# Layer 0 of a four-layer convolution stack: affine in the first pass, v multiplied with pixels on partitions, 32x32 turns, eight-tile output product

## The chip, the core and the metric

The kernel runs on one core of a Trainium2 chip. A core has five engines that run side by side, each with its own in-order queue: TensorE (PE; it loads weights and streams a moving operand past them, and writes to PSUM), VectorE (DVE), ScalarE (ACT), GpSimd (POOL) and SyncE (SP, here only a queue that starts DMAs). They meet only at semaphores. PSUM is the memory that TensorE writes to; SBUF is the working memory, with 128 partitions; HBM holds tensors between passes. The metric is the time of one execution on the device in microseconds (us), lower is better.

## What is computed

The input is a batch of 4 images with 48 channels and 256 x 256 pixels, in float32. Each of four layers adds a block to its input, `x = x + block(groupnorm(x))`. The change is in layer 0:

```python
hidden = _conv2d(x, w_hidden, b_hidden)                       # 48 -> 288 channels, 1x1
qkv = _conv2d(hidden, w_dw, b_dw, groups=C6, padding='SAME')  # 3x3, each channel alone
q, k, v = jnp.split(qkv, 3, axis=1)                           # 96 channels each
q_fft, k_fft = rfft2(q_patch), rfft2(k_patch)                 # 8x8 patches
out = irfft2(q_fft * k_fft)
mu  = jnp.mean(out, axis=1, keepdims=True)                    # over the 96 channels
var = jnp.var(out, axis=1, keepdims=True)
normed = (out - mu) / jnp.sqrt(var + EPS) * gamma + beta
return _conv2d(v * normed, w_out, b_out)                      # 96 -> 48 channels
```

Layers 1 and 2 are a gated convolution with a mask on the spectrum of 8x8 patches, layer 3 is a pooled gate. They are the same in both kernels.

## The kernel before

Layer 0 (the function `layer0`) works on strips of 16 image rows: 4 images x 16 strips are 64 steps. It goes over all strips twice.

**First pass (q and k).** A step n does, in the order of the source: `mixed(n)` (L377 on), the hidden product, 16 groups of eight matmuls, each group copied from PSUM into the tile `z` by ScalarE and VectorE in turn (L396); `arrange(n+1)` and `load(n+2)` on GpSimd, which bring the next strips; `attend(n-2)`; and `convolve(n)`, the 3x3 taps as matmuls (L408) whose results ScalarE copies (L463) and SP sends out to be rearranged into patches. `attend` handles the strip of two steps before, in two halves r = 0 and 1: spectra of q (`queries`, L512) and of k, multiplied on VectorE (`keys`, L517), the inverse transform (`inverse`, L527), copied into the tile `o` (L531). Then the normalization over channels: `centre(r)` sums on VectorE (L542), scales the sum (L543) and subtracts the mean on GpSimd (L544); `scale(r)` squares on ScalarE (L549), sums on VectorE (L551, L552), takes the power -1/2 on GpSimd (L553), multiplies on GpSimd (L554) and stores the strip to HBM as `kept` (L555). `centre(0)` stands between two units of `attend`; the rest is put between the groups of `convolve`: the dictionary that `attend` returns names, by pair (m, q), what follows the copy of group q of part m. Two things decide the order on an engine's queue: normally a planner orders the instructions before the run by readiness and source order, and `keep_in_program_order` (called `here` or `pin`) ties an instruction behind the one in front of it on its engine.

**Second pass (v).** A step n does `mixed(n)` for the 96 channels of v (8 groups), `arrange(n+1)`, then for strip n-1: `normalized` turns the kept strip with TensorE so that channels lie on partitions (L652), and ScalarE applies gamma and beta while copying (L657); `times_v` turns v in the same way (L669) and multiplies on VectorE (L675); `project` is the product with `w_out` (L685), added to the input strip `xt` with the bias on VectorE (L690), followed by the statistics for the next layer's norm (L694) and the store (L699). `convolve_v(n)` (L408, copy L639) stands between them. `load_kept` (L632, on SP) fetches the kept strip, two buffers; `load` (L335, on GpSimd) fetches an input strip, three buffers. A PSUM tile of two banks is used throughout, with four of them in rotation.

Of the kernel before, what the change touches and what calls it, by code (L numbers as in the profile page):

```python
# [17 lines left out]
C = 48  # L18
# [155 lines left out]
def conv_stack_kernel(ctx: ExitStack, tc: tile.TileContext, t: dict):  # L174
# [71 lines left out]
    def layer0():  # L246
# [8 lines left out]
        kept = [dram.tile([2, 128, C2, 16], F32, tag=f"n_{n}", name=f"n_{n}") for n in range(N)]  # L255
# [15 lines left out]
        class Strips:  # L271
# [104 lines left out]
            def mixed(self, n):  # L376
# [5 lines left out]
                to = self.z[0:PX].rearrange("p c (h u j) -> p h c u j", h=2, u=2)  # L382
                for u in range(2):
                    for j0 in range(0, NJ, per):
# [10 lines left out]
                        copy = nc.scalar.copy if (j0 // per) % 2 == 0 else nc.vector.tensor_copy  # L395
# [19 lines left out]
        with ExitStack() as st:  # L415
# [32 lines left out]
            qk = Strips("qk", 0, 2, 1, wp, sb, psum, ("f", 2), 1)  # L448
            patches = {}
# [38 lines left out]
            def attend(n):  # L488
# [30 lines left out]
                def inverse(i):  # L519
                    r, ch = units[i]  # L520
                    f = fs.pop(i)
                    if ch == 0:
                        os_[r] = sb.tile([128, C2, 16], F32, tag="o", name=f"o_{n}_{r}", bufs=2)
                    ps = qk.ps2(f"o_ps_{n}_{i}")
                    for e in range(2):
# [6 lines left out]
                        os_[r].rearrange("p (e c) q -> p e (c q)", e=2)[:, :, 384 * ch : 384 * ch + 384],  # L532
                        ps[:, :, 0:384],
                    )

                over = lambda v: v.rearrange("p (c q) -> p c q", c=1).to_broadcast([128, C2, 16])
                by_q = lambda v: v.rearrange("p c q -> p q c")
                small_ = lambda k, r: sb.tile([128, 16], F32, tag=k, name=f"{k}_{n}_{r}", bufs=2)

                def centre(r):  # L540
                    mu = small_("mu", r)
                    here(nc.vector.tensor_reduce(mu, by_q(os_[r]), AX.X, ALU.add))  # L542
                    nc.vector.tensor_scalar(mu, mu, 1.0 / C2, None, ALU.mult)  # L543
                    here(nc.gpsimd.tensor_tensor(os_[r], os_[r], over(mu), ALU.subtract))  # L544

                def scale(r):
                    o = os_[r]
                    sq = sb.tile([128, C2, 16], F32, tag="f", name=f"sq_{n}_{r}", bufs=2)
                    here(nc.scalar.activation(sq, o, AF.Square))  # L549
                    var = small_("var", r)  # L550
                    here(nc.vector.tensor_reduce(var, by_q(sq), AX.X, ALU.add))  # L551
                    nc.vector.tensor_scalar(var, var, 1.0 / C2, LN_EPS, ALU.mult, ALU.add)  # L552
                    here(nc.gpsimd.tensor_tensor(var, var, neg_half, ALU.pow))  # L553
                    nc.gpsimd.tensor_tensor(o, o, over(var), ALU.mult)  # L554
                    nc.gpsimd.dma_start(kept[n][r], o)  # L555
# [3 lines left out]
                for i in range(4):  # L559
# [9 lines left out]
                    (1, 0): lambda: scale(1),  # L569
# [31 lines left out]
        with ExitStack() as st:  # L601
# [3 lines left out]
            w_out = wp.tile([HC, 64], F32, tag="l0_w_out", name="l0_w_out")  # L605
            nc.gpsimd.memset(w_out, 0.0)

            affine = wp.tile([HC, 3], F32, tag="l0_affine", name="l0_affine")
            nc.gpsimd.memset(affine, 0.0)
            for h in range(2):  # L610
                at, ch = slice(64 * h, 64 * h + C), slice(C * h, C * h + C)
                nc.scalar.dma_start(w_out[at, :C], t["l0_w_out"][ch])
                for k, name in enumerate(("l0_gamma", "l0_beta")):
                    nc.scalar.dma_start(affine[at, k : k + 1], t[name][0:1, ch].rearrange("o c -> c o"))
                nc.scalar.dma_start(affine[at, 2:3], t["l0_b_out"])
            v = Strips("v", 2 * C2, 1, 0, wp, sb, psum, ("nt", 4), 3)

            ss = [wp.tile([128, 64, 64], F32, tag=f"s{i}", name=f"s_v_{i}") for i in range(2)]
            for s in ss:
                nc.gpsimd.memset(s[:, :, 48:64], 0.0)  # L620
# [5 lines left out]
            for w in ws:  # L626
                nc.gpsimd.memset(w[:, :, C:64, :], 0.0)
# [788 lines left out]
```

## Time and profile before

| | us |
|---|---|
| time, median of 3 runs (12357.9 to 12379.25) | 12371.74 |
| the profiled execution | 12404.2 |
| its span | 12402.4 |
| TensorE matmul busy | 11483.6 (93%) |
| VectorE busy | 8003.2 (65%) |
| ScalarE busy | 5857.8 (47%) |
| GpSimd busy | 3566.2 (29%) |
| first pass of layer 0, first hidden product to last | 129.8 to 2949.9 |
| second pass of layer 0, the same | 3099.6 to 4942.8 |

The profile records one execution. A row of a group names the line of the kernel, the engine, the operation and the tiles, and gives its busy time and the mean duration of one instruction; "PEld" is TensorE's weight load, which overlaps the matmuls. Each matmul of the source appears as two instructions. The timeline lists instructions in order of start, neighbours of one kind merged ("x2"), with the idle time in front of them and what ended it. The clock is that which the chip granted TensorE, as a share of full speed.

### The profile page before, as it was taken

Reading aid. Unit: us, or ns where it says so; the run is one execution under the profiler, and the core shown is the slowest. Engines: PE = TensorE matmul, PEld = TensorE weight load, DVE = VectorE, ACT = ScalarE, POOL = GpSimd, SP = SyncE. Lnnn points to the kernel's source line nnn. Section 1 sums busy time; section 2 is a strip of 40 time slices with the busy share of each in tenths; the row PEclk is TensorE's granted clock in tenths of the full one; section 3 lists DMA queues with packets and bytes.
Section 4 is the critical chain, followed back from the end, with each engine's and each line's share of the span. In section 5 each row is a group of like instructions: output and inputs, shape, how many; then the busy total and the mean of one; then the engine's idle time right before and its main releaser. Section 6 shows DMA issues by size and latency. Waiting matters only on the chain. (4 is left out here: it accounts for less than half of the span.)

```text
span 12402.4 us, 457165 instructions
## 1 busy us (share of the span) xinstructions
PE 11483.6 (93%) x209364; PEld 9013.2 (73%) x209364; DVE 8003.2 (65%) x8422; ACT 5857.8 (47%) x7294; POOL 3566.2 (29%) x4300
## 2 busy tenths in 40 slices
PE   5789999997999999999999999999999999999975
PEld 3567777775888888677777777777777777777764
DVE  4667666665444444576666666666766666766778
ACT  2355555554434334444444444444444444444456
POOL 3456666665222222212112112111111121121111
PEclk9899999998999999999999999998999999999987
DMA  6666666665444444455554555554555545555556
GB/s 165 196 206 215 211 216 213 211 217 173 114 118 115 115 112 113 92 118 113 118 118 100 116 116 114 114 116 88 117 109 115 117 100 112 117 115 112 117 142 198
DMA packets 379730, 1707.67 MB, mean 138 GB/s; under 512 B 100193, under 2 KB 102098, under 8 KB 281810
## 3 DMA queue, kind: packets, MB, share of 16 engines
q1 hardware_dynamic: 203016, 907.70, 27.6%
q0 software_dynamic: 130176, 630.91, 21.5%
q10 hardware_dynamic: 44618, 139.81, 4.8%
q8 instruction: 1651, 27.05, 0.9%
q14 instruction: 269, 2.20, 0.1%
HBM read 832.52 MB, written 584.91 MB: 114 GB/s over the span
## 5 line engine op out<-in xcount | busy, mean ns | idle before, releaser
L996 PEld LDWEIGHTS c_ps<-z,d 100*64 100x64 f32 x76032 | 2354.6, 140 | 501.5 <-issue 183.1
L996 PE MATMUL c_ps<-z,d 100*64 100x64 f32 x76032 | 2461.2, 224 | 139.8 <-DVE res L1041 58.9
L1002 ACT ACTIVATE g<-c_ps 128x512 f32<-128x512 f32 x1188 | 686.8, 596 | 3114.8 <-PE c_ps L996 3064.9
L927 DVE TENSOR_TENSOR yf<-y_ps,mask 128x768 f32<-128x768 f32 x1536 | 1375.7, 952 | 688.7 <-PE y_ps L923 688.6
L923 PE MATMUL y_ps<-w_in,f 49*128 49x96 f32 x24576 | 1487.9, 277 | 17.3 <-issue 11.5
L923 PEld LDWEIGHTS y_ps<-w_in,f 49*128 49x128 f32 x24576 | 1422.3, 190 | 56.7 <-issue 15.0
L1003 DVE TENSOR_TENSOR g<-g,c_ps 128x512 f32<-128x512 f32 x1188 | 793.1, 684 | 975.4 <-ACT g L1002 974.7
L974 POOL DMA_DIRECT2D z<-z x384 | 197.6, 515 | 3839.7 <-ACT z L967 3739.2
L949 PE MATMUL z_ps<-yf,dft 64*64 64x512 f32 x9216 | 1099.1, 604 | 7.2 <-DVE yf L927 5.6
L967 ACT COPY z<-z_ps 64x1024 f32<-64x1024 f32 x1024 | 1074.8, 1075 | 34.1 <-DVE z L967 10.1
L959 ACT COPY z<-z_ps 64x512 f32<-64x512 f32 x1536 | 857.9, 611 | 230.5 <-PE z_ps L949 209.7
L1007 DVE STREAM_TRANSPOSE g<-g 128x2048 f32<-128x2048 f32 x396 | 911.2, 2301 | 4.9
L1033 PE MATMUL xo_ps<-g,w_out 24*64 24x512 f32 x12288 | 846.4, 599 | 28.7 <-ACT z L967 28.1
L408 PEld LDWEIGHTS c_ps_qk<-z_qk,d_qk 109*64 109x64 f32 x24576 | 785.1, 139 | 50.5 <-issue 38.2
L389 PE MATMUL h_ps_qk<-w_qk,xn_qk 49*108 49x192 f32 x8192 | 739.6, 336 | 77.0 <-DVE z_qk L396 68.7
L967 DVE COPY z<-z_ps 64x1024 f32<-64x1024 f32 x512 | 619.3, 1210 | 296.6 <-PE z_ps L949 274.4
L408 PE MATMUL c_ps_qk<-z_qk,d_qk 109*64 109x64 f32 x24576 | 795.9, 224 | 11.9 <-issue 7.9
L500 PE MATMUL f_ps<-t,l_fft 64*94 64x384 f32 x4096 | 753.2, 504 | 27.3 <-ACT f L512 21.1
L389 PEld LDWEIGHTS h_ps_qk<-w_qk,xn_qk 49*108 49x108 f32 x8192 | 685.9, 176 | 116.7 <-DVE z_qk L396 92.2
L544 POOL TENSOR_TENSOR o<-o,mu 128x1536 f32<-128x1536 f32 x128 | 443.4, 3464 | 1079.5 <-DVE mu L543 812.5
L1041 DVE TENSOR_TENSOR res<-xo_ps,res 112x1024 f32<-112x1024 f32 x512 | 615.2, 1222 | 186.8 <-PE xo_ps L1033 159.2
L1033 PEld LDWEIGHTS xo_ps<-g,w_out 24*64 24x64 f32 x12288 | 301.0, 131 | 562.3 <-issue 220.3
(205 smaller groups left out, 17192.2 us busy)
## 6 DMA issues: line engine op xcount, KB each, us to landing
z<-z SPq DMA_DIRECT2D x1152, 203.9 KB
t<-s SPq DMA_DIRECT2D x512, 384.0 KB
t<-t SPq DMA_DIRECT2D x256, 768.0 KB
n<-o POOLq DMA_DIRECT2D x128, 768.0 KB, 5.0
kept<-n SPq DMA_DIRECT2D x128, 768.0 KB
xf<-x ACTq DMA_DIRECT2D x256, 384.0 KB
res<-x POOLq DMA_DIRECT2D x248, 384.0 KB, 6.2
x<-res POOLq DMA_DIRECT2D x248, 384.0 KB, 4.3
```

Of the source, the lines that this page charges most:

```text
L389: nc.tensor.matmul(ps[0:PX, h, nch * j : nch * j + nch], self.xn[at, u, j0 + j].rearrange("p r c -> p (r c)"), self.w1[at, self.c_first : ...
L408: nc.tensor.matmul(ps[64 * e : 64 * e + 64, k // 8, 64 * (k % 8) : 64 * (k % 8) + 64], self.d[:, 96 * m + c, :], self.z[:, 96 * m + c, :], ...
L500: nc.tensor.matmul(ps[0:94, e, 0:384], fft[at, 0:94], patches[n, m, r][at, rp, 24 * ch : 24 * ch + 24, :].rearrange("p c u -> p (c u)"), s ...
L923: first(i + j == 0, nc.tensor.matmul(ps[:, i, 96 * j : 96 * j + 96], f[at, 4 * h + j, :], w_in[at, m, :], start=True, stop=True,))
L927: pin(nc.vector.tensor_tensor(y[:, :, :, 4 * h : 4 * h + 4], ps[:, :, 0:384].rearrange("p i (j c) -> p c i j", j=4), mask[:, m].rearrange( ...
L949: first(q == 2 and p + v == 0, nc.tensor.matmul(to[64 * v : 64 * v + 64], dft[at, 1, at], y[at, c0 : c0 + 16].rearrange("p c i j -> p (c i ...
L959: pin(nc.scalar.copy(columns(p, 48 * v + 32, 48 * v + 48), last[64 * v : 64 * v + 64, p].rearrange("p (c i j) -> p c i j", i=2, j=16),))
L967: pin(copy(columns(p, 48 * v, 48 * v + 32), ps[64 * v : 64 * v + 64].rearrange("p q (c i j) -> p (q c) i j", i=2, j=16),))
L996: first(v + k == 0, nc.tensor.matmul(ps[p0 : p0 + 64, v, f0 : f0 + nj], d[rows, HID * v + 48 * m + c, :], z[rows, us, 48 * v + c, 1 : NP + ...
L1003: pin(nc.vector.tensor_tensor(to, to, of[:, 1], ALU.mult))
L1007: pin(nc.vector.transpose(flat, flat))
L1033: first(i + k == 0, nc.tensor.matmul(ps[h][k // 2][64 * i : 64 * i + 64, k % 2, :], w_out[at, m, :], gs[m][at, j0 : j0 + 16].rearrange("p ...
```

## The change

In the first pass the tile `o` is laid out as [half of the channels, pixel group, channel] instead of [channel, pixel group], so that the sums run over neighbouring elements; each sum is made in two halves and added. `scale` no longer multiplies. A new function `affine` does what was left and what the second pass did with gamma: 16 instructions of VectorE per half multiply `o` by the power and by gamma, GpSimd adds beta, and then the strip is stored. The dictionary has four entries instead of two.

In the second pass v is multiplied as it leaves PSUM, with pixels on partitions, by the kept strip (now fetched in that layout, by eight DMAs instead of two, three buffers); VectorE turns the product in blocks of 32x32; and `project` is made of products with 32 and 16 rows that use different parts of the TensorE array. `normalized` and `times_v` are gone. The statistics move to the end of the step, `load_kept` ahead of `convolve_v`, the image's mean behind `mixed`, and all copies of `mixed` go to ScalarE. The diff, cut to its core:

```diff
-                to = self.z[0:PX].rearrange("p c (h u j) -> p h c u j", h=2, u=2)
+                to = self.z[0:PX].rearrange("p c (u h j) -> p h c u j", h=2, u=2)
...
-                        copy = nc.scalar.copy if (j0 // per) % 2 == 0 else nc.vector.tensor_copy
+                        shared = self.thirds == 1 or (j0 // per) % 2 == 0
+                        copy = nc.scalar.copy if shared else nc.vector.tensor_copy
...
-                        os_[r] = sb.tile([128, C2, 16], F32, tag="o", name=f"o_{n}_{r}", bufs=2)
+                        os_[r] = sb.tile([128, 2, 16, C], F32, tag="o", name=f"o_{n}_{r}", bufs=2)
...
+                def total(k, r, of):
+                    halves = sb.tile([128, 2, 16], F32, tag="halves", name=f"{k}2_{n}_{r}", bufs=2)
+                    here(nc.vector.tensor_reduce(halves, of, AX.X, ALU.add))
+                    v = small_(k, r)
+                    here(nc.vector.tensor_tensor(v, halves[:, 0], halves[:, 1], ALU.add))
+                    return v
+
                 def centre(r):
-                    mu = small_("mu", r)
-                    here(nc.vector.tensor_reduce(mu, by_q(os_[r]), AX.X, ALU.add))
-                    nc.vector.tensor_scalar(mu, mu, 1.0 / C2, None, ALU.mult)
+                    mu = total("mu", r, os_[r])
+                    here(nc.vector.tensor_scalar(mu, mu, 1.0 / C2, None, ALU.mult))
                     here(nc.gpsimd.tensor_tensor(os_[r], os_[r], over(mu), ALU.subtract))
 
+                vars_ = {}
+
                 def scale(r):
...
+                    sq = sb.tile(all_, F32, tag="f", name=f"sq_{n}_{r}", bufs=2)
+                    here(nc.scalar.activation(sq, os_[r], AF.Square))
+                    vars_[r] = var = total("var", r, sq)
+                    here(nc.vector.tensor_scalar(var, var, 1.0 / C2, LN_EPS, ALU.mult, ALU.add))
                     here(nc.gpsimd.tensor_tensor(var, var, neg_half, ALU.pow))
-                    nc.gpsimd.tensor_tensor(o, o, over(var), ALU.mult)
+
+                def affine(r):
+                    o, var = os_[r], vars_.pop(r)
+                    for q in range(16):
+                        here(nc.vector.scalar_tensor_tensor(
+                            o[:, :, q], o[:, :, q], var[:, q : q + 1], gain, ALU.mult, ALU.mult
+                        ))
+                    here(nc.gpsimd.tensor_tensor(
+                        o, o, shift.rearrange("p (e q) c -> p e q c", q=1).to_broadcast(all_), ALU.add
+                    ))
                     nc.gpsimd.dma_start(kept[n][r], o)
...
                     (0, 0): lambda: (centre(1), scale(0)),
-                    (1, 0): lambda: scale(1),
+                    (0, 2): lambda: scale(1),
+                    (1, 0): lambda: affine(0),
+                    (1, 2): lambda: affine(1),
...
+            gvs = [wp.tile([128, 64, 64], F32, tag=f"gv{i}", name=f"gv_{i}") for i in range(2)]
+            for gv in gvs:
+                nc.gpsimd.memset(gv, 0.0)
...
                     for e in range(2):
-                        nc.sync.dma_start(
-                            ws[n % 2][:, :, 64 * e : 64 * e + C, :],
-                            kept[n].rearrange("r p c q -> p r c q")[:, :, C * e : C * e + C, :],
-                        )
+                        for r in range(4):
+                            nc.sync.dma_start(
+                                ws[n % 3][64 * e + 16 * r : 64 * e + 16 * r + 16].rearrange(
+                                    "x j q c -> x j (q c)"
+                                ),
+                                kept[n][r // 2, 64 * (r % 2) : 64 * (r % 2) + 64, e].rearrange(
+                                    "(j x) q c -> x j (q c)", x=16
+                                ),
+                            )
...
             def convolve_v(n):
+                gv = gvs[n % 2].rearrange("p (q j) c -> p j q c", j=4)
+
                 def put(q, ps):
...
+                    at = slice(16 * q, 16 * q + 16)
+                    pin(nc.vector.tensor_tensor(
+                        gv[:, :, :, at], ps.rearrange("p k (c q j) -> p j q (k c)", q=16, j=4),
+                        ws[n % 3][:, :, :, at], ALU.mult,
+                    ))
...
+                for u in range(2):
+                    flat = gvs[n % 2][:, 32 * u : 32 * u + 32].rearrange("p b c -> p (b c)")
+                    pin(nc.vector.transpose(flat, flat))
+
+            def project(n, u):
...
+                ps = [v.ps2(f"y_ps_{n}_{u}_{e}") for e in range(2)]
                 for k in range(2):
                     for h in range(2):
...
+                        for f in range(2):
+                            for e in range(2):
+                                p0 = 32 * (2 * e + f)
+                                at = slice(p0, p0 + (32, 16)[k])
+                                ins = nc.tensor.matmul(
+                                    ps[e][64 * h : 64 * h + 64, f, :], w_out[at, k, :],
+                                    gv[at, b0 : b0 + 16, 32 * k : 32 * k + 32].rearrange(
+                                        "p j (r x) -> p r j x", x=16
+                                    ),
+                                    start=(k == 0), stop=(k == 1),
+                                )
...
+                pin(nc.vector.scalar_tensor_tensor(
+                    at, ps[0][:HC].rearrange("p k f -> p (k f)"), b_out, at, ALU.add, ALU.add
+                ))
+                pin(nc.vector.tensor_tensor(
+                    at, ps[1][:HC].rearrange("p k f -> p (k f)"), at, ALU.add
+                ))
...
+            def take_stats(n):
...
+                for k in range(4):
+                    pin(nc.vector.bn_stats(
+                        out_stats[b][:, 4 * s + k, :], rows[:, 512 * k : 512 * k + 512]
+                    ))
...
             for n in range(N + 1):
+                if n < N:
+                    v.mixed(n)
+                    v.arrange(n + 1)
                 if moments:
                     ps = v.ps2(f"gn1_ps_{n}_mean")
                     moments = gn_mean(moments, ps[:, 0], f"l1_{len(coefs)}")
...
                 if n >= 1:
...
+                    for u in range(2):
+                        project(n - 1, u)
+                load_kept(n + 2)
                 if n < N:
                     convolve_v(n)
...
                 if n >= 1:
-                    project(n - 1, 1, nts2)
+                    take_stats(n - 1)
...
-                load_kept(n + 1)
                 v.load(n + 2)
```

## The prediction

> **What bounds the kernel now.** The page's chain of waits covers a quarter of the span and none of layer 0, so it can't be used here. I read the slices for the clock, then the table of windows for a steady stretch of each pass of layer 0, then the timeline of one step in each. Layers 1 to 3 are untouched and keep their time.
>
> ```profile
> 1240.00:2480.00 1240.00, 1184.28 (x18025) 896.60 (x18023) 859.01 (x730) 721.50 (x833) 773.19 (x489) 1.00 0.64 213
> 3128.40:4760.00 1631.60, 1558.39 (x34623) 1368.56 (x34618) 763.76 (x807) 655.47 (x835) 399.31 (x684) 0.98 0.46 116
> ```
>
> The columns are busy time of TensorE matmul, weight load, VectorE, ScalarE and GpSimd, then clock, DMA share, GB/s. TensorE is busy 95.5% of both passes, at full clock. First pass: a step lasts 41.36 us (the centring L544 starts at 1758.88, 1800.22, 1841.59). Second pass: (4936.6 - 3099.6) / 63 = 29.16 us. The second pass is bound by TensorE alone; in the first, VectorE ends two waits. One step of it, not in order of engine:
>
> ```profile
> 1804.43 2.86 DVE L542 TENSOR_REDUCE mu<-o 128x16 f32<-128x1536 f32 x1 [2.63 <-ACT o L531]
> 1807.63 3.49 POOL L544 TENSOR_TENSOR o<-o,mu 128x1536 f32<-128x1536 f32 x1 [3.97 <-ACT sq L549]
> 1810.37 0.79 DVE L552 TENSOR_SCALAR var<-var 128x16 f32<-128x16 f32 x1
> 1814.26 3.46 POOL L554 TENSOR_TENSOR o<-o,var 128x1536 f32<-128x1536 f32 x1
> 1815.92 1.83 DVE L552 TENSOR_SCALAR var<-var 128x16 f32<-128x16 f32 x1
> 1817.67 2.91 DVE L396 COPY z_qk<-h_ps_qk 108x768 f32<-108x768 f32 x3
> 1818.67 7.40 PE L389 MATMUL h_ps_qk<-w_qk,xn_qk 49*108 49x192 f32 x88 [0.89 <-DVE z_qk L396]
> ```
>
> Start, duration, engine, work, and in brackets idle time and its releaser. VectorE works off the normalization of one strip and only then reaches the copies L396 that TensorE needs for the next strip's hidden product: TensorE already waits 0.9 us for them. And L552, 16 numbers, lasts 0.79 and 1.83 us although its twin L543 lasts 0.17: both times it ends where a GpSimd operation ends (1811.12, 1817.72).
>
> **First pass, part by part.** I count from the end of the last product of spectra (L517, 1801.80). Before: first L396 copy at +15.9, next such end at +41.4.
>
> *Reductions.* The sums now run over neighbouring channels. Row L1259 has 2048 elements in 2277 ns, L1260 has 512 in 688 ns: 1536 cost 1.75 us instead of 2.80, plus a small add of 0.17. Four per step save some 3.5 us of VectorE, but only the one in front of the last L517 is on the path: that pair can start at most 0.65 us earlier, since its second operand leaves TensorE at 1841.58. Gain 0.65.
>
> *Chain to the affine.* Mean of the second half done at +4.8, centring (3.49) to +8.4, its square to +10.0, its total and scalar to +12.2. The first half's power (L553, 2.94) runs +8.9 to +11.8, the second's starts at +12.3.
>
> *Affine.* 32 scalar_tensor_tensor of 96 elements per step. Nearest rows: L690 with 1024 elements, 1284 ns, and
>
> ```profile
> L1299 DVE SCALAR_TENSOR_TENSOR a<-xp,l,a 112x512 f32<-112x512 f32 x32 | 23.9, 747 | 0.3
> ```
>
> 1.05 ns an element and 210 ns fixed: 0.31 us each; neighbours overlap a little (two L517 of 0.946 take 1.81), so 0.24 to 0.31. Sixteen cost 3.9 to 5.0; I take 4.2, nearer to the overlapped end because they are independent. The multiplication L554 becomes an addition of the same size, 3.46.
>
> *The lock.* The Trainium skill, "SBUF — State Buffer", section "Who interferes with whom", says that VectorE and GpSimd hold a shared port pair exclusively for a whole instruction, and that a VectorE instruction with two SBUF inputs contends with a GpSimd one that reads SBUF. L552 above shows such blocking for a scalar operation; no row shows it for two inputs. By the rows alone, both affines end at 12.2 + 8.4 = +20.6. By the rule, the second power (2.94) stands against the first affine, and the first shift (3.46) against the second. Whoever wins, the power comes in front of one of the two affines; the shift comes between or not. So +23.6 to +27; I take the rule and the middle, 12.2 + 2.9 + 4.2 + 1.7 + 4.2 = +25.2.
>
> *Who is queued behind.* The L396 copies of the next strip stand after the affine in the source; in the trace they follow the last L552 as in the source, and what slips past them (statistics L433) does so in gaps. So I take source order. Eight of sixteen groups go through VectorE; TensorE has four buffers, so it does five to eight groups and stops. Copies start at +25.2 instead of +15.9: 9.3 us later.
>
> *Clock.* That gap (about +17 to +26) lies in the middle of TensorE's work. A similar gap exists in the trace, where an image begins:
>
> ```profile
> 3726.41 6.32 PE L389 MATMUL h_ps_v<-w_v,xn_v 49*108 49x96 f32 x128
> ...
> 4055.31 0.51 PE L209 MATMUL gn_ps_mean<-mv_l,c_gmean 112*112 112x1 f32 x2 [4.71 <-DVE mv_l L203]
> 4055.74 11.84 PE L389 MATMUL h_ps_v<-w_v,xn_v 49*108 49x96 f32 x128
> ```
> ```profile
> 4055.00:4058.00 3.00, 2.69 (x26) 2.71 (x28) 0.80 (x5) 0.40 (x1) 1.04 (x2) 0.50 0.46 104
> ```
>
> After 4.71 us of idling the clock is 0.50 and the same 128 products take 11.84 instead of 6.32; it is 1.00 again only at 4072. After the idle 9 us at 2984 it is half for 7 us. Gaps of 2.4 us (at 3741) did not do it. The Trainium skill, "TensorE: Matmul & The Clock Gate", Part 1, gives one idle window of some 3.4 us for the drop and one busy window for the return: by that the rest costs 1.7 us more, by the rows 3.5 (7 us at half rate) to 6.4 (all eleven groups). The rows decide; 4.5.
>
> Step: 9.3 + 4.5 - 0.65 = +13.2 us. It occurs where both normalization and a next strip exist, 61 times: +805 us. The drain after the last strip (two normalizations with nothing beside them) and two memsets of 4096 columns: +15. Sum +820, between +450 and +1000.
>
> *At nothing.* The first output copy writes 768 elements in another order: L463 reads PSUM strided at the same rate (1024 in 1.01, L531 768 in 0.80). The normalized strip is stored behind the affine, some 9 us later than now; it lands in 5 us, and its buffer is next written a strip later, after the copies that are just as late. Without that cover the output copies would wait.
>
> **Second pass, part by part.** Removed from TensorE per step: transposes L652 (2048 matmuls, 260.8 us in all: 4.1 a step) and turning v:
>
> ```profile
> L669 PE MATMUL v_ps<-ident,s_v 64*64 64x64 f32 x8192 | 506.0, 219 | 7.0 <-issue 7.0
> L669 PE MATMUL v_ps<-ident,s_v 64*48 64x64 f32 x8192 | 495.3, 218 | 0.0
> L1033 PE MATMUL xo_ps<-g,w_out 24*64 24x512 f32 x12288 | 846.4, 599 | 28.7 <-ACT z L967 28.1
> ```
>
> (7.9 a step in the timeline.) Output product: now 4.0 a step (L685, 253.7 / 64), new 64 instructions in the tiling of L1033, whose rate is 846.4 / 12288 = 69 ns: 4.4. Left: hidden product 6.3, taps 5.8, output 4.4 = 16.5 us.
>
> Others per step. VectorE: three products from PSUM 3.7 (L675, 1.22), two turns of 2048 4.6 (L1007, 2.30), two adds per half 5.0 (1.28 + 1.22), statistics 2.6: 15.9. ScalarE has all eight copies of the hidden product, 6.4, beside TensorE's 6.3. GpSimd as before. SP issues eight loads of 0.36 instead of two, 2.9, with nothing else in its queue. The image's mean moves behind the hidden product: the 4.7 us idle above goes three times, but the mean then waits behind the turns, so I count nothing. None of VectorE's has two SBUF inputs.
>
> But a load now waits later. It overwrites the strip that the statistics read, and these stand behind the turns: end of taps + 1.35 (last product) + 4.5 + 2.6, so 8.5 us later. Then:
>
> ```profile
> 3731.41 0.52 POOL L335 DMA_DIRECT2D x_v<-in_x  x1 [2.28 <-DVE z_v L396]
> ...
> 3740.00 1.49 POOL L347 COPY xn_v<-x_v 113x1536 f32<-113x1536 f32 x1 [7.32 <-DMA x_v<-in_x]
> ```
>
> 8.6 us to land, 2.1 to arrange the first half, and the product after next can start: (16.6 + 8.5 + 8.6 + 2.1) / 2 = 17.9. Through GpSimd's queue: load 8.6, arrange 4.1, four stores 2.1 to issue and 3.7 to land, next load: 18.5; 2 more if the load runs at the first pass's landing (8.3 against 6.3 median), since it now overlaps the normalized strip's. I take 19.3, between 18 and 22. Gain 9.9 x 63 = 624 (450 to 700).
>
> **Sum.** +820 - 624 = +196 on the profiled execution (span 12402.4, 12404.2 with what lies around it). That run is 0.26% above the median 12371.74, to which I add the difference: **12570 us**, 1.6% slower.
>
> **Rivals.** (1) *The copies overtake the affine.* The order is planned ahead, and in the first 700 us statistics (L433) are seen slipping between the copies. Against: they only fill gaps, and the affine's 32 instructions are ready together. If so, VectorE has 28.7 - 3.5 + 8.6 = 33.8 us of work and up to 6.4 of blocking in 41: +150 us, and 12372 + 150 - 624 = 11900. (2) *No lock for two inputs*: copies at +20.6, +4.7 a step, gap near the limit for the clock, 61 x 4.1 = 250 with none of it: 12000; half clock would take it to 12250. (3) *The second pass gains little*: strips now come by eight loads into 16 neighbouring partitions each. No row shows that form. Now they use 16.3% of a step's DMA time, 4.8 us, beside 8.4 of the other queue; at four times the price 19 + 8.4 = 27 us a step, no gain; decided from 19 us on. At 24 us: 12372 + 820 - 325 = 12870.
>
> **How the numbers follow.** Main case 0.64, own range 12330 to 12800; rival 1 0.15, rival 2 0.09, rival 3 0.12. Two tenths of a per cent (25 us) is what can be told from no change. In the main case 0.83 are slower, 0.04 equal; rivals 1 and 2 are faster, 3 slower: slower 0.65, same 0.04, faster 0.31. The range 11950 to 12850 leaves out the better half of rival 1 and the worse half of 3.
>
> **What would show it.** Right: steps of some 54 us in the first pass, an idle TensorE of 8 us inside L389 released by L396 copies, clock below 0.9 there, stretched scalar_tensor_tensor beside GpSimd; 19 us steps in the second. Wrong: L396 ahead of the affine in VectorE's queue, sixteen affine instructions in 4 us beside a power, or a second pass held by the loads of the kept strip.

## The result and the profile after

The changed kernel takes 12544.85 us (median of 4 runs, 12536.27 to 12555.33) beside 12368.82 us for the kernel before on the same chip: 1.0143 times as long (95% interval 1.0125 to 1.0160). The forecast, 12570 us, is 25 us away. The total is right by luck. It is made of two wrong numbers: the first pass cost a third of what I forecast, the second gained a sixth, and the two errors nearly cancelled.

The profiled spans are 12402.4 us before and 12546.5 after, 144.1 us apart. In these two executions the first hidden product of the second pass starts at 3099.6 before and at 3379.5 after, and the last one at 4942.8 and 5121.3. So everything up to the second pass costs 279.9 us more (forecast 820), the second pass 1741.8 us instead of 1843.2, 101.4 less (forecast 624), and the rest 34.4 less. Of that rest, 14 us lie between the last hidden product and layer 1, in the last strip's remaining work, which has no turns by TensorE any more; the other 20 lie in layers whose code is the same, and their cause stays open.

The table of windows of the changed kernel, for a steady stretch of each pass (busy time of TensorE matmul, weight load, VectorE, ScalarE, GpSimd, then clock, DMA share, GB/s):

```profile
1240.00:2480.00 1240.00, 1126.63 (x16325) 867.62 (x16323) 823.53 (x1627) 649.00 (x746) 744.58 (x437) 0.94 0.58 191
3410.00:4700.00 1290.00, 1055.28 (x17956) 825.72 (x17942) 726.91 (x635) 296.52 (x374) 334.10 (x577) 0.73 0.76 123
```

Before, both rows had TensorE busy 95.5% of the time at a clock of 0.98 to 1.00. Now the second pass has it busy 82% at a clock of 0.73, and the DMA share went from 0.46 to 0.76. TensorE lost work there, and used the room to wait and to run slowly.

**One step of the first pass.** The timeline of the changed kernel, from the centring of a strip's second half on (start, duration, engine, work, idle time and its releaser); the last product of spectra before it ended at 1801.19:

```profile
1806.06 2.77 POOL L554 TENSOR_TENSOR o<-o,mu 128x1536 f32<-128x1536 f32 x1 [4.20 <-ACT s L467]
...
1809.15 2.93 POOL L563 TENSOR_TENSOR var<-var,neg_half 128x16 f32<-128x16 f32 x1 [0.32 <-DVE var L562]
...
1812.69 7.42 DVE L568 SCALAR_TENSOR_TENSOR o<-o,var,l_gain 128x96 f32<-128x96 f32 x32
1812.86 2.91 POOL L563 TENSOR_TENSOR var<-var,neg_half 128x16 f32<-128x16 f32 x1 [0.78 <-DVE var L562]
1816.59 6.82 POOL L571 TENSOR_TENSOR o<-o,l_shift 128x1536 f32<-128x1536 f32 x1 [0.81 <-DVE o L568]
1820.03 2.68 DVE L397 COPY z_qk<-h_ps_qk 108x768 f32<-108x768 f32 x3
1821.04 9.70 PE L389 MATMUL h_ps_qk<-w_qk,xn_qk 49*108 49x192 f32 x80 [3.21 <-DVE z_qk L397]
1824.36 3.45 POOL L571 TENSOR_TENSOR o<-o,l_shift 128x1536 f32<-128x1536 f32 x1
```

All 32 scalar_tensor_tensor run in one block of 7.42 us, 0.232 us each, while a power (L563) and an addition (L571) of GpSimd run beside them. The power takes 2.91 us there and 2.93 before the block: it loses nothing. The addition takes 6.82 us there and 3.45 us alone. It starts 3.5 us before the block ends and takes 3.4 us longer, as if it had stood until the block was over. So there is contention between the two engines, but it is GpSimd that yields. The copies L397 start at 1820.03, 18.8 us after the product of spectra; the forecast was 25.2, and 20.6 without the lock. TensorE stands for 3.21 us, from 1817.8 on, and comes back with half its clock, as three rows of the windows of this step show (the last number but two is the clock; 0.87 over the first 3 us means half speed from 1820.2 on):

```profile
1818.00:1821.00 3.00, 0.00 (x0) 0.00 (x0) 3.00 (x12) 0.04 (x1) 3.00 (x1) 0.87 0.65 256
1821.00:1825.00 4.00, 3.96 (x24) 3.81 (x26) 2.67 (x3) 0.83 (x1) 3.68 (x3) 0.50 0.06 23
1825.00:1830.00 5.00, 5.00 (x52) 4.92 (x50) 2.44 (x3) 2.48 (x3) 4.70 (x4) 0.79 0.51 210
```

The centring L554 starts at 1799.11 and again at 1845.45: the step is 46.3 us instead of 41.36.

**One step of the second pass**, hidden product L389, ScalarE's first copy L397 and output product L687 of the changed kernel:

```profile
4023.61 1.00 PE L389 MATMUL h_ps_v<-w_v,xn_v 49*108 49x96 f32 x16
...
4024.72 0.80 ACT L397 COPY z_v<-h_ps_v 108x768 f32<-108x768 f32 x1 [12.37 <-PE h_ps_v L389]
...
4025.57 1.00 PE L389 MATMUL h_ps_v<-w_v,xn_v 49*108 49x96 f32 x16 [0.95 <-ACT z_v L397]
...
4029.48 1.76 PE L389 MATMUL h_ps_v<-w_v,xn_v 49*108 49x96 f32 x16 [0.95 <-ACT z_v L397]
...
4032.28 1.76 PE L389 MATMUL h_ps_v<-w_v,xn_v 49*108 49x96 f32 x16 [1.04 <-ACT z_v L397]
...
4034.99 4.64 PE L389 MATMUL h_ps_v<-w_v,xn_v 49*108 49x96 f32 x48 [0.94 <-ACT z_v L397]
...
4039.55 5.02 PE L687 MATMUL y_ps<-gv,l_w_out 32*64 32x512 f32 x64
```
```profile
4023.00:4028.00 5.00, 3.09 (x65) 2.70 (x63) 4.25 (x3) 1.60 (x2) 1.54 (x5) 1.00 0.67 151
4031.00:4040.00 9.00, 7.01 (x76) 6.27 (x80) 0.84 (x2) 3.47 (x5) 1.03 (x2) 0.50 1.06 151
```

A group of 16 instructions takes 1.00 us, and the next starts only when ScalarE has emptied the one before. I read that as one free PSUM buffer used by turns; the run ring, below, tests it. After some 5 us of working half the time (from 4023.6; the clock is 0.83 in the microsecond from 4028 and 0.50 in the next) the clock is 0.50, though no single gap exceeds 1.05 us, and the same 16 take 1.76. The hidden product lasts 16 us where the forecast had 6.3.

### The profile page after: what moved, and what is told of

Read it like the earlier page. It is cut to its first block, busy times and chain, and to the rows that moved or that the text cites. A ratio compares the mean times of both kernels' runs of the same rounds, so it can differ in the third digit from the quotient of the medians.

```text
span 12546.5 us, 428535 instructions
## 1 busy us (share of the span) xinstructions
PE 11264.8 (90%) x194004; PEld 8673.5 (69%) x194004; DVE 8232.6 (66%) x10662; ACT 5505.2 (44%) x6846; POOL 3670.0 (29%) x4298
## 5 line engine op out<-in xcount | busy, mean ns | idle before, releaser
L389 PE MATMUL h_ps_qk<-w_qk,xn_qk 49*108 49x192 f32 x8192 | 867.7, 375 | 230.5 <-DVE z_qk L397 220.0
L389 PEld LDWEIGHTS h_ps_qk<-w_qk,xn_qk 49*108 49x108 f32 x8192 | 800.6, 202 | 284.0 <-DVE z_qk L397 250.6
L389 PE MATMUL h_ps_v<-w_v,xn_v 49*108 49x96 f32 x8192 | 720.7, 349 | 303.7 <-ACT z_v L397 270.9
L397 ACT COPY z_v<-h_ps_v 108x768 f32<-108x768 f32 x512 | 407.6, 798 | 1319.6 <-PE h_ps_v L389 1319.3
L389 PEld LDWEIGHTS h_ps_v<-w_v,xn_v 49*108 49x108 f32 x8192 | 649.9, 253 | 366.0 <-ACT z_v L397 261.0
```

The costliest lines, as they stand in the source:

```text
L389: nc.tensor.matmul(ps[0:PX, h, nch * j : nch * j + nch], self.xn[at, u, j0 + j].rearrange("p r c -> p (r c)"), self.w1[at, self.c_first : ...
```

## The experiments

Eleven kernels, each the changed kernel with one to three things altered; times are medians of 3 to 20 runs, of nogain one run. "Second pass" is the time from the start of its first hidden product to the last instruction of its last one, divided by 63 steps, from the profiled execution; it was 29.26 us before and is 27.65 us in the changed kernel. (The last product's own length lies in it. From product to product, as the prediction counted, it is 29.16 before and 27.40 after.)

| run | median us | ratio to before, 95% interval | second pass, us a step |
|---|---|---|---|
| nogain (left out: product with gain) | 12216.83, one run | none | 27.7 |
| noshift (left out: addition of beta) | 12522.11 | 1.0129 (1.0110 to 1.0148) | 27.7 |
| split | 12691.81 | 1.0272 (1.0257 to 1.0287) | 27.7 |
| own | 12972.06 | 1.0496 (1.0478 to 1.0513) | 34.5 |
| alt | 13075.31 | 1.0576 (1.0559 to 1.0594) | 35.9 |
| own_pin | 12439.19 | 1.0057 (1.0037 to 1.0077) | 26.4 |
| own_loads | 12340.49 | 0.9983 (0.9976 to 0.9990) | 25.1 |
| own_loads_x4 | 12326.03 | 0.9962 (0.9947 to 0.9977) | 24.3 |
| ring | 12370.73 | 1.0003 (0.9993 to 1.0013) | 24.9 |
| loads | 12236.00 | 0.9901 (0.9886 to 0.9916) | 22.7 |
| loads_x4 | 12185.79 | 0.9855 (0.9836 to 0.9874) | 22.1 |

### The first pass

**noshift**: is VectorE held by GpSimd?

```diff
-                    here(nc.gpsimd.tensor_tensor(
-                        o, o, shift.rearrange("p (e q) c -> p e q c", q=1).to_broadcast(all_), ALU.add
-                    ))
```

> The changed kernel without GpSimd's addition of beta in the first pass (that addition is left out, so beta is missing in the output; the store follows VectorE's 32 instructions). Theory from the trace after (GpSimd gives way: its addition takes 6.8 us beside VectorE's instructions instead of 3.5, and VectorE's 32 take 0.232 us each either way): copies of the hidden product start where they did, the first pass is the same within 0.7 us a step, total 12500 to 12560. Rival (the prediction's: VectorE is held while GpSimd's two-input addition runs): VectorE's instructions end some 4 us earlier in every step, total 12250 to 12320.

Measured 12522.11 us, where the trace had it and 200 us from what the prediction's lock asks. The second pass starts at 3347.3 instead of 3379.5, half a microsecond a step. With GpSimd's addition gone, VectorE's block is as long as with it (timeline of noshift):

```profile
1841.12 7.42 DVE L568 SCALAR_TENSOR_TENSOR o<-o,var,l_gain 128x96 f32<-128x96 f32 x32
1848.46 1.81 DVE L397 COPY z_qk<-h_ps_qk 108x768 f32<-108x768 f32 x2
```

So the addition cost VectorE nothing that can be seen: 7.42 us both times. The power still runs here, but in the changed kernel the 32 instructions follow each other at the same pace beside the power and beside the addition (229 ns from start to start, the median of all steps).

**nogain**: does the longer first pass come from the 32 instructions?

```diff
-                    for q in range(16):
-                        here(nc.vector.scalar_tensor_tensor(
-                            o[:, :, q], o[:, :, q], var[:, q : q + 1], gain, ALU.mult, ALU.mult
-                        ))
```

> The changed kernel without the 32 VectorE instructions of the first pass (left out: the product with the reciprocal deviation and with gamma, so the kept strip is only centred and shifted). Theory (all of the first pass's 5 us a step is VectorE's block of 7.4 us ahead of the copies of the hidden product, and the lower clock after it): first pass back to 41 to 42 us a step, total 12200 to 12280. Rival (the longer first pass comes from the other layout, its reductions and centring or the strip's store): 12450 or more.

Measured 12216.83 us, in one run, as the theory had it; the second pass starts at 3034.2, 345 us earlier than in the changed kernel and 65 earlier than before the change. The group of the hidden product in the window 1240 to 2480 us, in the changed kernel (instructions, then busy time, mean ns of one, and the idle time before them with what ended it), after the same group of the kernel before:

```profile
L389 PE MATMUL h_ps_qk<-w_qk,xn_qk 49*108 49x192 f32 x3728 | 317.1, 325 | 23.6 <-DVE z_qk L396 21.9 <-ACT w_qk L374 1.7
```
```profile
L389 PE MATMUL h_ps_qk<-w_qk,xn_qk 49*108 49x192 f32 x3456 | 363.4, 374 | 95.5 <-DVE z_qk L397 94.0 <-ACT w_qk L374 0.8 <-issue 0.6
```

and in nogain:

```profile
L389 PE MATMUL h_ps_qk<-w_qk,xn_qk 49*108 49x192 f32 x3968 | 330.7, 324 | 2.0 <-ACT w_qk L374 1.7 <-issue 0.3
```

A step has 128 of them, so the window holds 29 steps in the kernel before, 27 in the changed kernel and 31 in nogain. The wait of 3.5 us a step for the copies goes entirely, and the product itself falls from 13.5 to 10.7 us as the clock stays up. Together these are 6.3 us, slightly more than the 5.9 by which the step shrinks (1240 / 27 to 1240 / 31, that is to 40.0 us and a little under the theory's 41); nothing else is needed. The run takes away both the block's place in the queue and its work. That it is the place is read from the trace: VectorE is busy two thirds of the window, and TensorE's wait ends with the copies behind the block.

**split**: half of the block taken out of the copies' way.

```diff
+                        if not shared:
+                            tc.keep_in_program_order(ins)
+                            for work in self.late[:2]:
+                                work()
+                            del self.late[:2]
...
+                    if r == 1 and n + 3 < N:
+                        qk.late = works
```

> The changed kernel, but in the first pass only the affine of the strip's first half stays in one block of 16 VectorE instructions; those of the second half are put two behind each VectorE copy of the next strip's hidden product, and its addition of beta and its store follow them. The same instructions in number. Theory (what the affine costs is that the copies of the hidden product queue behind 32 instructions of 0.232 us, and TensorE starts again at a low clock): copies start 3.7 us earlier, eight pairs of 0.46 us lie in the gaps between copies that wait for TensorE, the step falls from about 46.5 to 42.5 to 44 us, total 12300 to 12420. Rival (VectorE's whole work in a step, or its port shared with GpSimd, sets the step): no change, 12500 to 12590, because VectorE has the same work to do.

Measured 12691.81 us: neither, so the question of place or work stays without an experiment. The copies did start earlier, and TensorE's wait for them in the window fell to 59.1 us in 25 steps (from 94.0 in 27), but a new wait took its place (groups of split in the same window):

```profile
L418 PE MATMUL c_ps_qk<-z_qk,d_qk 109*64 109x64 f32 x9600 | 327.8, 232 | 75.7 <-ACT o L544 73.7 <-issue 1.9
...
L544 ACT COPY o<-o_ps 128x768 f32<-128x768 f32 x102 | 81.4, 798 | 254.3 <-DMA n<-o 135.2 <-PE o_ps L540 100.3 <-issue 18.1
```

The strip's store now leaves later and lands in 8.0 us instead of 3.6, and the buffer `o` is wanted by the next strip's output copies; TensorE stands behind those, 3 us a step. It is the wait that the prediction named as the price if the store's cover were gone. More buffers for `o` were not tried.

### The second pass

**own**: two PSUM buffers for the hidden product alone.

```diff
-                return self.psum.tile([128, 2, 512], F32, tag="ps2", name=name)
...
+                if self.thirds == 2:
+                    return self.psum.tile([128, 2, 512], F32, tag="ps2", name=name)
+                return self.psum.tile([128, 2, 512], F32, tag="h" if hidden else "ps2", name=name, bufs=2)
...
```

> The changed kernel, but in its second pass the hidden product h_ps_v has two PSUM buffers of its own and all the other products share the other two, instead of all four being handed out in turn. Theory (one buffer in turn, then a clock at half): in the changed kernel six of the eight groups of the hidden product each wait for ScalarE to empty the group before, the product takes 16 us instead of 6.3, and TensorE's clock falls to 0.5 there. With two buffers the product takes about 7 us, the granted clock of the second pass rises from 0.73 to above 0.9, the step falls from about 27.6 to 19 to 21 us, and the total is 11960 to 12150 us. Rival (the kept loads into 16 partitions at a time limit the step): the step stays at 25 us or more and the total at 12390 or more, with VectorE's products waiting for a DMA instead.

Measured 12972.06 us: by the number in the rival's range, but not for its reason, since VectorE's products wait for the taps and for no DMA (388.7 us before L668 in the window 3560 to 4600). The edit moved more than I meant. With a buffer free early, the planned order put two groups of the next strip's hidden product ahead of the taps (timeline of own):

```profile
4013.75 0.52 POOL L337 DMA_DIRECT2D x_v<-in_x  x1 [15.39 <-DVE stats L715]
...
4027.03 1.49 POOL L349 COPY xn_v<-x_v 113x1536 f32<-113x1536 f32 x1 [9.31 <-DMA x_v<-in_x]
...
4029.13 2.11 PE L391 MATMUL h_ps_v<-w_v,xn_v 49*108 49x96 f32 x18 [10.50 <-POOL xn_v L356]
...
4031.18 5.61 PE L411 MATMUL c_ps_v<-z_v,d_v 109*64 109x64 f32 x128
...
4045.46 2.43 DVE L715 BATCH_NORM_STATS2 stats<-x_v 112x6 f32<-112x512 f32 x4
```

Read as a ring: the load waits for the statistics, the hidden product for the load, the taps stand in TensorE's queue behind that product, and the next statistics wait for the taps. The ring closes once a step, 34.5 us. In the changed kernel the taps come first, and by the same reading the ring has two steps to go round.

**alt**: copies of the hidden product by both engines again.

```diff
-                        shared = self.thirds == 1 or (j0 // per) % 2 == 0
+                        shared = (j0 // per) % 2 == 0
```

> The changed kernel, but the copies of the hidden product in the second pass alternate between ScalarE and VectorE as they did before the change; the buffers are as in the changed kernel. Theory (one buffer in turn): a group still waits for the copy of the group before, whichever engine makes it, so the product stays at 12 to 16 us, the clock below 0.85, and the total within 100 us of 12545. Rival (ScalarE alone is too slow for eight copies in a row): the product falls to 6 to 7 us and the step by about 9 us, total 11970.

Measured 13075.31 us, neither. The groups still wait in turn, as expected, but VectorE's products of the strip before now stand behind its copies (timeline of alt):

```profile
4030.24 0.96 DVE L397 COPY z_v<-h_ps_v 108x768 f32<-108x768 f32 x1 [4.58 <-PE h_ps_v L389]
4031.11 3.47 DVE L666 TENSOR_TENSOR gv<-c_ps_v,kept 128x1024 f32<-128x1024 f32 x3
...
4039.87 2.43 DVE L713 BATCH_NORM_STATS2 stats<-x_v 112x6 f32<-112x512 f32 x4
...
4042.59 1.03 POOL L335 DMA_DIRECT2D x_v<-in_x  x2 [19.45 <-DVE stats L713]
...
4054.64 1.49 POOL L347 COPY xn_v<-x_v 113x1536 f32<-113x1536 f32 x1 [7.65 <-DMA x_v<-in_x]
```

Again the ring closes within one step. That all eight copies lie on ScalarE, as the change has it, is worth 4.3% here (1.0576 / 1.0143).

**own_pin**: own buffers, with the order kept.

```diff
+                                if self.thirds == 1 and (u, j0 + j, h) in ((0, 0, 0), (1, NJ - 1, 1)):
+                                    tc.keep_in_program_order(ins)
...
+                            if self.thirds == 1 and (q, k, e) in ((0, 0, 0), (2, 15, 1)):
+                                tc.keep_in_program_order(ins)
```

> As the run with two PSUM buffers for the hidden product, but TensorE keeps the changed kernel's order (taps of a strip, hidden product of the next, output product), where that run put two groups of the next hidden product ahead of the taps, so that TensorE stood for 10.5 us of a 34.5 us step on an input load with the taps behind it. Loads of the kept strip into 16 partitions, as in the changed kernel. Theory (two bounds close to each other: the serial hidden product makes a step of 16.0 + 5.0 + 7.3 us, and the ring of the input load, landing 12, arranging 4, hidden product 7, output 5, taps 7, products, transposes and statistics 8, is 43 to 44 us for two strips): the step falls from 27.6 to about 22 us and the total to 12150 to 12250. Rival (the kept loads alone limit, the buffers do not matter): 12450 to 12600.

Measured 12439.19 us: just under its rival's range. The hidden product is no longer serial, yet the gain is a quarter to a third of what the theory asked. The other two buffers are too few (groups of own_pin, 43 steps):

```profile
L413 PE MATMUL c_ps_v<-z_v,d_v 109*64 109x64 f32 x8256 | 316.4, 251 | 82.8 <-DVE x_v L703 64.9 <-issue 17.9
...
L693 PE MATMUL y_ps<-gv,l_w_out 32*64 32x512 f32 x1367 | 176.5, 786 | 71.7 <-DVE x_v L703 63.9 <-DVE x_v L706 7.8
```

The second half of the output product and the taps each wait some 1.5 us for VectorE to empty the output buffers. The new output product holds two buffers at once, twice in a row, and then the taps want three.

**own_loads**: the same, and loads of the kept strip into 64 partitions each.

```diff
-                        for r in range(4):
+                        for j in range(4):
                             nc.sync.dma_start(
-                                ws[n % 3][64 * e + 16 * r : 64 * e + 16 * r + 16].rearrange(
-                                    "x j q c -> x j (q c)"
-                                ),
+                                ws[n % 3][64 * e : 64 * e + 64, j].rearrange("p q c -> p (q c)"),
...
```

> The run before it (own buffers, order of the changed kernel) with the kept strip loaded into 64 partitions by each DMA. Theory (the ring of the input load is what is left, and its landing shortens from 11 to 12 us to 9): two strips take 3 us less in the ring, the step is 20 to 21 us, total 12050 to 12130, that is 60 to 120 us under the run with loads into 16 partitions. Rival (TensorE's own work limits, 17 to 18 us a step): no difference between the two, both near 11950. Rival (the loads were the whole of the 309 us that they gave alone): 12236 again, the buffers giving nothing more.

Measured 12340.49 us, 99 us below own_pin: the difference is as the theory had it, the total is not, because own_pin's waits stay. This is the cleanest price of the loads: same order, same buffers. The way that the theory gave is not shown, though: the input, which was to land sooner, takes 10.3 us to land in own_pin and 10.0 here (medians of the window 3560 to 4700).

**loads**: the same loads on the changed kernel itself.

> The changed kernel, but the kept strip is loaded by eight DMAs into 64 partitions each (one for each of two halves and four columns of the tile, runs of 3 KB) instead of eight into 16 partitions each. Same bytes. Theory (the loads are hidden behind the hidden product): the queue's time for a strip falls from 11 us towards the 4.75 us that the same bytes took before the change, and the total stays within 60 us of 12545. Rival (the loads limit the step, 0.12 in the prediction): the step falls by 3 us or more, total below 12350.

Measured 12236.00 us, and my theory that the loads were hidden fell. The DMA queues in the window 3560 to 4700 us (share of 16 engines; last column of the second line, us to land), before:

```profile
q1 hardware_dynamic: 21096, 61.03, 16.6%
...
x_v<-in_x POOLq DMA_DIRECT2D x72, 480.0 KB, 6.6
```

in the changed kernel:

```profile
q1 hardware_dynamic: 25902, 63.70, 40.5%
...
x_v<-in_x POOLq DMA_DIRECT2D x74, 480.0 KB, 11.2
```

and in loads:

```profile
q1 hardware_dynamic: 27314, 78.98, 20.1%
...
x_v<-in_x POOLq DMA_DIRECT2D x95, 480.0 KB, 9.2
```

The same bytes cost 2.3 times the queue time by eight loads into 16 partitions (40.5% of 27.65 us a step against 16.6% of 29.26), and with 64 partitions nearly what they cost before (20.1% of 22.67, 4.6 us). But this run also has another handing-out of PSUM buffers: its hidden product never waits for ScalarE. The 309 us are therefore not all of the loads.

**ring**: PSUM buffers in strict rotation, loads as in the changed kernel.

```diff
-                return self.psum.tile([128, 2, 512], F32, tag="ps2", name=name)
+                if self.thirds == 2:
+                    return self.psum.tile([128, 2, 512], F32, tag="ps2", name=name)
+                self.turn = (self.turn + 1) % 4
+                return self.psum.tile([128, 2, 512], F32, tag=f"ps{self.turn}", name=name, bufs=1)
```

> The changed kernel, but in its second pass the four PSUM buffers are handed out strictly in rotation, tile after tile, instead of as the planner estimates that they come free; loads into 16 partitions as in the changed kernel. With that the first groups of a hidden product stand on the buffers of the taps of the strip before, and later groups on four buffers in rotation. Question: the run with loads into 64 partitions also got another handing-out of buffers, since the planner's estimates moved. Theory (that was two thirds of its 309 us; loads alone gave 99 us between two runs with the same buffers): the hidden product falls from 16 to 7 to 12 us, total 12290 to 12380. Rival (the shape of the loads was all of it): 12500 to 12560.

Measured 12370.73 us, inside the theory's range: the handing-out of four buffers alone is worth 1.4% and brings the kernel level with the one before. TensorE's idle time in front of the hidden product for ScalarE falls from 270.9 to 44.4 us in the whole pass. These are TensorE's waits before the hidden product that ScalarE ended (us, times), in the changed kernel and in ring:

```profile
  ACT z_v L397: 270.9, 279
```
```profile
  ACT z_v L401: 44.4, 42
```

The 1.0% between ring and loads is not all the shape of the loads either, since the buffers are handed out differently in these two as well.

**loads_x4 and own_loads_x4**: a fourth input buffer.

```diff
-            v = Strips("v", 2 * C2, 1, 0, wp, sb, psum, ("basis", 2), 3)
+            v = Strips("v", 2 * C2, 1, 0, wp, sb, psum, ("basis", 2), 4)
```

> The run before it with a fourth buffer for the input of the second pass, so that a load waits for the statistics of four strips before and not of three. Theory (ring of the input load): the wait of GpSimd for the input load goes, and the step falls to TensorE's or VectorE's own work, 17 to 19 us (hidden 6.3, taps 5.8, output 4.4 and short waits), total 11900 to 12010. Rival (DMA share or the stores limit): as the run before within 40 us.

> The run with loads into 64 partitions, and a fourth buffer for the input of the second pass. Theory (with that run GpSimd waits 9 us of a 22.8 us step for the input load, and TensorE 2.7 us for GpSimd): those waits go, TensorE's clock there rises above 0.85, the step falls to 19 to 21 us, total 11990 to 12130. Rival (the waits lie beside TensorE's own work at its lower clock): 12190 to 12250.

In the first of the two texts the run before is own_loads. Measured 12326.03 us, 14 below own_loads, far from the theory's 12010 and within its rival's 40 us, and 12185.79 us, 50 below loads: just under its rival's range, and not what the theory asked. GpSimd's wait for the input did go in both (in own_loads_x4, before its copy L349, from 426.3 to 0.4 us in the window 3560 to 4600), and other waits took its place: in own_loads_x4 those of own_pin, so not the DMA share or the stores that the rival named, in loads_x4 this one (its groups from 3560 to 4600 us, 46 steps):

```profile
L389 PE MATMUL h_ps_v<-w_v,xn_v 49*108 49x96 f32 x5938 | 411.1, 313 | 137.6 <-DVE gv L664 136.5 <-POOL w_scale_v L364 0.5
...
L664 DVE TENSOR_TENSOR gv<-c_ps_v,kept 128x1024 f32<-128x1024 f32 x141 | 165.1, 1218 | 197.1 <-DMA kept<-n 187.0 <-PE c_ps_v L409 6.2 <-PE h_ps_v L389 3.6
```

VectorE waits for the kept strip to land, 4 us a step, and holds the buffers for which the hidden product waits. Whether a fourth buffer for the kept strip ends that was not tried. Of all versions loads_x4 is the fastest: 1.45% below the kernel before (interval 1.26 to 1.64%), with the whole computation in place.

## Why the prediction came out, point by point

**First pass, +13.2 us a step forecast, some +5 measured.** *Reductions*: 1.75 us, exact. *Chain*: the second half's total and scalar at +12.2 forecast, 1812.78 - 1801.19 = +11.6 measured; the centring took 2.77 us and not 3.49. *Affine*: 32 in 7.42 us, 3.7 for sixteen, just under my lower end of 3.9. *The lock* is the step that failed. I let the rule of the Trainium skill ("SBUF — State Buffer", "Who interferes with whom") add 4.6 us to what the rows gave, 2.9 for the power and 1.7 for the addition. The power ran beside the block without a cost to either side; the addition met contention, but only GpSimd paid for it, 6.82 against 3.45 us, and noshift shows VectorE's block equally long without it. By the rows alone I had +20.6; the trace has +18.8. *Clock*: 4.5 us forecast. The drop came, 2.4 us into a standstill of 3.21 instead of 8, though the prediction had a gap of 2.4 us that did nothing. It cost 13.5 - 10.9 = 2.6 us of longer products (10.9 from the 317.1 us that the 3728 instructions took before). That is under the 3.5 to 6.4 that I had read from my rows and over the 1.7 that I had estimated by the clock rule that the next paragraph names. Together, 2.6 of clock and 3.5 - 0.8 = 2.7 of waiting make about the 5. The mechanism, copies queued behind the affine and a TensorE that comes back slow, is what the trace and nogain show; its size was too large by 8 us a step, 4.6 of them the lock. The sign that I had named for being wrong, sixteen affine instructions in 4 us beside a power, is there; the steps of 54 us and the stretched instructions of VectorE are not.

**Second pass, -9.9 us a step forecast, -1.6 measured.** The forecast of 19.3 us was the ring of the input load, with TensorE's work counted as 16.5 us and so hidden beneath it. In the changed kernel's window 3560 to 4600 us,

```profile
3560.00:4600.00 1040.00, 852.39 (x14248) 662.94 (x14254) 574.22 (x505) 237.84 (x299) 267.37 (x462) 0.72 0.76 121
```

TensorE is busy 852.39 of 1040 us, 22.7 of a 27.65 us step, and idle 5.0. So some 6.2 us are the clock (22.7 times the granted 0.72 is 16.3, near the 16.5 counted) and 5.0 are waits, 4.3 of them (270.9 / 63) for ScalarE inside the hidden product. The step that failed is "ScalarE has all eight copies, 6.4, beside TensorE's 6.3": beside holds only if a second buffer is free, and I counted the buffers in the first pass and not in the second. The copy and the group then add up, TensorE works half the time, and the clock halves. (The table of two states in the Trainium skill, "TensorE: Matmul & The Clock Gate", Part 1, which the prediction set against its rows, gives one idle window of some 3.4 us for the drop; read as a gap of that length, it would have kept the clock up here, where no gap is longer than 1.05. The measurement decides.) The ring was mis-sized too: the input, put at 8.6 us to land, took 11.2. Since the ring lies close behind (own and alt close it within a step), removing one bound gave only part: ring 2.8 us a step, the loads by themselves 1.4 (own_pin to own_loads), both at once, in loads, 5.0, with the input buffer 5.5. The 19.3 us of the forecast were never reached; 22.1 is the best measured, with a fourth input buffer and hardly a wait for the input's landing, and what is left there is the wait for the kept strip.

**Rivals.** (1) The copies did not overtake the affine. (2) No lock for two inputs is true of VectorE, and with it the forecast would have been 12000 to 12250, further off: the right correction to one wrong term alone would have spoiled the sum. (3) The loads into 16 partitions do cost time, at 2.3 times the queue time and not four; I priced them as a bound from 19 us of queue time on, and 10.0 us of it (37.7% of 26.44 us in own_pin) already cost 99 us in time (own_pin against own_loads). How is not shown. In the changed kernel VectorE's products L666 wait for the taps and not for the kept strip (26.8 of 27.6 us of idle time, window 3560 to 4600). And the landing of the input does not follow the shape: it rose from 6.6 to 11.2, but is 8.4 in ring with the same loads and 9.2 in loads with the wider ones (same window as there). (The chances do not quite add up: the faster cases give 0.32 and not 0.31, the equal one 0.03.)

## What to carry to other kernels

Before counting two engines as side by side, count the buffers between them in that stage, with what the neighbouring tiles hold; with one free buffer "the longer of the two" becomes their sum, and here TensorE, at work half of the time, then lost its clock too. Where an engine falls idle for a dependence ring, ask how many steps the ring has to go round: an innocent edit that puts one instruction ahead of another in an in-order queue can halve that number, as I read own and alt. And split a forecast into terms that the trace can measure one by one: here the total was right and both terms were wrong, so the total alone would have taught nothing.

## What the hardware showed that I had not expected

- A dense run of two-input VectorE instructions (32 in 7.42 us) slows a two-input GpSimd addition from 3.45 to 6.82 us and is not slowed itself; a GpSimd power of 128x16 elements beside it is not slowed either (2.91 us, 2.93 without).
- TensorE's clock fell to 0.50 without any idle gap above 1.05 us, after some 5 us in which it worked half of the time (4023.6 to 4028.7).
- The same 1.5 MB a strip cost 11.2 us of queue time as eight loads into 16 partitions and 4.6 as eight into 64.
- Centring the same 128x1536 elements by GpSimd takes 2.77 us with one mean for a run of 96 neighbouring channels and 3.46 in the layout before, where the mean changes from one element to the next.
